# Attention and mixer on one core: half-width transform matmuls grouped, mixer engines kept in written order, MLP pieces rearranged

## The chip, the cores and the metric

The kernel runs on one core of a Trainium2 chip. The metric is device time in microseconds (us), from launch to the last output. Engines are named as the profile names them: PE (TensorE matmul), PEld (its weight load), DVE (VectorE), ACT (ScalarE), POOL (GpSimd) and SP (SyncE, which here only issues DMAs).

## The reference

Eight images of 128 x 128 pixels and 64 channels, float32, pass two layers.

```python
# layer 0: attention along the rows and columns of each pixel
Q, K, V = x @ w_q, x @ w_k, x @ w_v                  # Q, K: 8 channels
att = softmax(concat([Q.K along h (self masked), Q.K along w]))
x = gamma * (att_H V + att_W V) + x
# layer 1: Fourier mixer, then a convolutional MLP
F  = fft2(LN(x) @ w_te)                              # 64 -> 128 channels
fc = gelu(concat([F.re, F.im]) @ w_fc)
x1 = x + real(ifft2(fc.re + 1j * fc.im)) @ w_tp
h2 = LN(x1) @ w_fe                                   # 64 -> 128 channels
d  = gelu(depthwise_conv3x3(h2) + b_dw)
out = x1 + d @ w_fp
```

## The kernel before

**Two stages.** `attention` runs all eight images and writes its result to DRAM; `mixer` runs after it. The change is in the mixer.

**One image in the mixer.** `fourier(b)` transforms image b and leaves x1 in SBUF; `mlp(b)` makes the output from x1. While image b is transformed, the MLP of image b-1 runs beside it; image 0 has no MLP beside it, and the MLP of image 7 runs alone at the end. `fourier` yields after each of 36 steps of three kinds:

- W, 8 steps: transform along w for 8 channels (matmuls `aps`, L487) and a copy to `at` (ACT, L488).
- K, 19 steps over 17 groups of frequencies. Step i transforms group i along h (matmuls into `fps`, L499 to L507, copy `f` on ACT, L509), multiplies group i-1 by the channel weights (`fcps`, L522; gelu on ACT, L528; add or subtract on POOL, L529), and projects group i-2 back to 64 channels (`gps`, L549; copy `gt` on ACT, L552). Fifteen groups have 4 frequencies, one has 3, and the last holds the two real ones, 0 and 64.
- I, 9 steps over 8 blocks of 8 channels: inverse along h (`inverse_h`: matmuls `yps`, L576 to L580, copy `ys` on ACT, L581), then one step later inverse along w (`inverse_w`: matmuls `dps`, L587, and two additions into x1 on DVE, L593).

**A complex product.** For each frequency or channel one matmul has a full-width stationary operand of 128 columns (real and imaginary part of 64 channels) and two have half-width operands of 64 columns, which write the lower and the upper half of the partitions. A float32 matmul appears in the trace as two passes, so one such triple is six rows of PE.

**The MLP** goes through 16 chunks of 8 image rows. Of chunk k: `normed(k)` (POOL, L618), `transposed(k)` (four PE transposes `tpn`, L627, and an ACT copy `xtn`, L631), `expand(k)` (matmuls `hp`, L648, and ACT copies `h`, L642 and L653), nine `taps` of the 3x3 filter (tap 0 on ACT, L670; taps 1 to 8 on DVE, L672, all into one accumulator `acc`), `gelu(k)` (ACT, L679) and `shrink(k)` (POOL adds the bias to x1 in `ot`, L690; 8 matmuls `op`, L695; DVE adds them, L696; SP sends `ot` out, L697). `statistics(s)` takes mean and variance of 64 rows on DVE (L612) and ends with a square root on ACT (L71) and a reciprocal on DVE (L72). The MLP is a generator too; each `yield` ends a piece.

**What sets the order.** The main loop calls `next` on the MLP in proportion to the work done:

```python
        pieces = 4 + PIECES * (P // CH)
        work = W_STEP * 8 + K_STEP * (len(groups) + 2) + I_STEP * 9
        ...
                    while share < pieces * done / work:
                        next(before, None)
```

With weights 2, 7 and 5 the work of an image is 194, so a K step is followed by about three pieces and an I step by about two. After each I step two pieces of `load_norm(b+1)` follow (DMA `xl`, L470, and POOL `xn`, L471). This written order is not what the engines get: a scheduler reorders the instructions of every engine by its own estimate of when they are ready.

**Buffers.** PSUM in the mixer: two buffers for `fps`, `gps` and `yps`, two for `aps`, `fcps` and `dps`, and two (`ps_c`) for `tpn`, `op` and the two halves of `hp`. In SBUF most tiles have two buffers; `xn`, `at` and `gt` share two.

Of the kernel before, what the change touches and what calls it, by code (L numbers as in the profile page):

```python
# [21 lines left out]
F32 = mybir.dt.float32  # L22
BF16 = mybir.dt.bfloat16
AF = mybir.ActivationFunctionType
ALU = mybir.AluOpType
# [4 lines left out]
P = 128  # L30
C = 64
# [3 lines left out]
CH = 8  # L35
NORM_ROWS = 8

W_STEP, K_STEP, I_STEP = 2.0, 7.0, 5.0
PIECES = 5


def dft_tables():
# [321 lines left out]
def mixer(tc, nc, x2, scale1, tbl, prm, out):  # L364
# [3 lines left out]
    with ExitStack() as ctx:  # L368
# [111 lines left out]
        def fourier(b):  # L480
# [11 lines left out]
            for g in groups + [None, None]:  # L492
                nxt = None
                if g is not None:
                    fps = ps_m.tile([P, 4, P], F32, tag="mm", name="fps")
                    for n, k in enumerate(g):
                        if k % 64 == 0:
                            a = at[:, k // 64, :]
                            nc.tensor.matmul(fps[0:64, n, :], lhsT=a, rhs=cos, start=True, stop=True)  # L499
                            nc.tensor.matmul(fps[64:128, n, :], lhsT=a, rhs=nsin, start=True, stop=True)  # L500
                            continue
                        nc.tensor.matmul(  # L502
                            fps[:, n, :], lhsT=at[:, 2 * k : 2 * k + 2, :].rearrange("p t c -> p (t c)"), rhs=cos,
                            start=True, stop=False,
                        )
                        nc.tensor.matmul(fps[0:64, n, :], lhsT=at[:, 2 * k + 1, :], rhs=sin, start=False, stop=True)  # L506
                        nc.tensor.matmul(fps[64:128, n, :], lhsT=at[:, 2 * k, :], rhs=nsin, start=False, stop=True)  # L507
                    f = p2.tile([P, 4, P], F32, tag="f", name="f")
                    nc.scalar.copy(f[:, 0 : len(g), :], fps[:, 0 : len(g), :])  # L509
                    nxt = (g, f)  # L510
                tp_next = None
                if pend_fc is not None:
                    gg, f = pend_fc
                    n = len(gg) * P
                    fv = f.rearrange("p k h -> p (k h)")[:, 0:n]
                    gs = []
                    for half in range(2):
                        ps = ps_f.tile([P, 2, 512], F32, tag="fc", name="fcps")
                        cols = slice(half * HID, half * HID + HID)
                        for sgn, w in enumerate((wplus, wminus)):  # L520
                            mean = gg[0] == 0
                            nc.tensor.matmul(ps[:, sgn, 0:n], lhsT=w[:, cols], rhs=fv, start=True, stop=not mean)  # L522
                            if mean:
                                nc.tensor.matmul(
                                    ps[:, sgn, 0:1], lhsT=dc[:, cols], rhs=ident[0:1, 0:1], start=False, stop=True
                                )
                        gl = p2.tile([P, 2, 512], F32, tag="gl%d" % half, name="gl")
                        nc.scalar.activation(gl[:, :, 0:n], ps[:, :, 0:n], AF.Gelu, bias=bfc[:, half : half + 1])  # L528
                        nc.gpsimd.tensor_tensor(  # L529
                            gl[:, 0, 0:n], gl[:, 0, 0:n], gl[:, 1, 0:n], ALU.add if half == 0 else ALU.subtract  # L530
                        )
                        gs.append(gl)
                    tp_next = (gg, gs)
                if pend_tp is not None:
                    gg, (gr, gi) = pend_tp
                    gps = ps_m.tile([P, 4, 2, C], F32, tag="mm", name="gps")
                    if gg[0] == 0:

                        nc.tensor.matmul(gps[:, 0, 0, :], lhsT=gr[:, 0, 0:P], rhs=wtp, start=True, stop=False)
                        nc.tensor.matmul(gps[:, 0, 0, :], lhsT=gi[:, 0, P : 2 * P], rhs=wtpn, start=False, stop=False)  # L540
                        nc.tensor.matmul(gps[:, 0, 0, :], lhsT=e0, rhs=btp, start=False, stop=True)
                        nc.tensor.matmul(gps[:, 0, 1, :], lhsT=gi[:, 0, 0:P], rhs=wtp, start=True, stop=False)
                        nc.tensor.matmul(gps[:, 0, 1, :], lhsT=gr[:, 0, P : 2 * P], rhs=wtp, start=False, stop=True)
                        k0, n = 63, 1
                    else:
                        k0, n = gg[0] - 1, len(gg)
                        for j in range(n):
                            for t, src in enumerate((gr, gi)):
                                nc.tensor.matmul(  # L549
                                    gps[:, j, t, :], lhsT=src[:, 0, j * P : j * P + P], rhs=wtp, start=True, stop=True  # L550
                                )
                    nc.scalar.copy(gt[:, :, :, k0 : k0 + n], gps[:, 0:n, :, :].rearrange("p k t c -> p c t k"))  # L552
                pend_fc, pend_tp = nxt, tp_next
                yield K_STEP
# [15 lines left out]
        def inverse_h(gt, c0):  # L570
            ys = p2.tile([P, 8, P], F32, tag="ys", name="ys")
            for g in range(2):
                yps = ps_m.tile([P, 4, P], F32, tag="mm", name="yps")
                for n in range(4):
                    c = c0 + 4 * g + n
                    nc.tensor.matmul(  # L576
                        yps[:, n, :], lhsT=gt[:, c, :, :].rearrange("p t k -> p (t k)"), rhs=cos, start=True, stop=False
                    )
                    nc.tensor.matmul(yps[0:64, n, :], lhsT=gt[:, c, 1, :], rhs=nsin, start=False, stop=True)  # L579
                    nc.tensor.matmul(yps[64:128, n, :], lhsT=gt[:, c, 0, :], rhs=sin, start=False, stop=True)  # L580
                nc.scalar.copy(ys[:, 4 * g : 4 * g + 4, :], yps)  # L581
            return ys

# [18 lines left out]
        def mlp(b):  # L602
# [75 lines left out]
                av = accs[k][:, 0 : i1 - i0, :]  # L678
                nc.scalar.activation(av, av, AF.Gelu)  # L679

            def shrink(k):
                i0, i1 = span(k)
                acc = accs.pop(k)
                for a in range(0, i1 - i0, CH):
                    n = min(CH, i1 - i0 - a)
                    r0 = k * CH - 1 + i0 + a
                    ot = p2.tile([P, CH, C], F32, tag="ot", name="ot")
                    for o, rows in lines(xs, r0, r0 + n):
                        m = rows.shape[1]
                        nc.gpsimd.tensor_tensor(  # L690
                            ot[:, o : o + m, :], rows, bfp.unsqueeze(1).to_broadcast([P, m, C]), ALU.add
                        )
                    op = ps_c.tile([P, CH, C], F32, tag="mc", name="op")
                    for i in range(n):
                        nc.tensor.matmul(op[:, i, :], lhsT=acc[:, a + i, :], rhs=wfp, start=True, stop=True)  # L695
                    nc.vector.tensor_tensor(ot[:, 0:n, :], op[:, 0:n, :], ot[:, 0:n, :], ALU.add)  # L696
                    nc.sync.dma_start(  # L697
                        out=out[b, r0 : r0 + n, :, :].rearrange("h w c -> w h c"), in_=ot[:, 0:n, :]
                    )

            statistics(0)
            normed(0)
            normed(1)
            yield
            transposed(0)
            yield
            expand(0)
            taps(0, 0, 1)
            yield
            for k in range(n_ch):  # L710
                taps(k, 1, 4)
                yield
                if k > 0:
                    gelu(k - 1)
                if k == 4:
                    statistics(1)
                if k + 2 < n_ch:
                    normed(k + 2)
                yield
                taps(k, 4, 6)  # L720
                if k > 0:
                    shrink(k - 1)
                yield
                if k + 1 < n_ch:
                    transposed(k + 1)
                taps(k, 6, 9)
                yield
                if k + 1 < n_ch:
                    expand(k + 1)
                    taps(k + 1, 0, 1)  # L730
                yield
            gelu(n_ch - 1)
            shrink(n_ch - 1)
            yield

        pieces = 4 + PIECES * (P // CH)
        work = W_STEP * 8 + K_STEP * (len(groups) + 2) + I_STEP * 9
        for _ in load_norm(0):  # L740
            pass
# [19 lines left out]
def attention_mixer_kernel(ctx: ExitStack, tc: tile.TileContext, x, w_q, b_q, w_k, b_k, w_v, b_v, gamma, *rest):  # L761
# [5 lines left out]
    keep = ctx.enter_context(tc.tile_pool(name="keep", bufs=1))  # L767
    scale1 = keep.tile([P, NB, P], F32, tag="scale1", name="scale1")
    attention(tc, nc, x, w_q, b_q, w_k, b_k, w_v, b_v, gamma, x2, scale1)
    mixer(tc, nc, x2, scale1, tbl, prm, out)  # L770


_INS = [
# [29 lines left out]
```

## Time and profile before

| | us |
|---|---|
| median of 3 runs (lowest to highest) | 4361.75 (4358.06 to 4362.67) |
| the profiled execution, its own time | 4356.02 |
| its span, first to last instruction | 4354.3 |
| attention, until the mixer's first DFT matmul (`aps`) | 1808.7 |
| image 0 in the mixer (first `aps` of image 0 to that of image 1) | 220.7 |
| a later image (first `aps` of image 2 to that of image 3) | 294.6 |
| image 7 and the last MLP, to the end | 557.0 |

The profiled execution is 5.7 us under the median of the runs. Busy shares over the whole span are PE 86%, DVE 63%, POOL 40%, ACT 38%, but they mix the two stages. A row of a timeline gives start, duration, engine, line and shape. Ends of matmuls are modelled, so the rate of PE is read from one start to the next. A wait in a list is the idle time of an engine and what ended it. "PEclk" is the share of the TensorE clock that was granted.

### The profile page before, as it was taken

What the parts mean: (1) busy time and instruction counts of PE and PEld (TensorE: products, weight loads), DVE (VectorE), ACT (ScalarE), POOL (GpSimd) and SP (SyncE); (2) the same over time, 40 slices, a digit from 0 to 9 for tenths busy, and PEclk for the clock granted to TensorE, in tenths of its full rate; (3) what the DMA queues carried; (4) which work ended last, traced back from release to release, by engine and by line L of the source; (5) the groups of instructions that cost most, each with busy time, mean ns of one, the idle gap of its engine ahead of it and who ended that gap; (6) DMA issues with size and microseconds to landing.
All of it is one profiled execution on the core that took longest, in us unless ns stands there. A gap on an engine that the chain in (4) does not pass through costs nothing.

```text
span 4354.3 us, 77800 instructions
## 1 busy us (share of the span) xinstructions
PE 3734.6 (86%) x32742; PEld 2615.0 (60%) x32742; DVE 2753.9 (63%) x4392; ACT 1672.0 (38%) x2215; POOL 1733.9 (40%) x1601
## 2 busy tenths in 40 slices
PE   7979797979897976499989989899899899899634
PEld 4665767666766665366656656566566566666423
DVE  4353545454545454104878878888878789788776
ACT  1405050505041412143635535536445355265222
POOL 0142424242424244333562554635725636344121
PEclk7859585858585857699989989999899899999755
DMA  3132322323232322401121111120211211200000
GB/s 91 44 106 56 105 78 83 89 72 96 67 101 60 100 56 67 144 6 35 37 54 32 37 51 35 51 57 15 73 35 35 54 34 42 61 14 16 13 17 20
DMA packets 452064, 243.92 MB, mean 56 GB/s; under 512 B 415874, under 2 KB 420354, under 8 KB 445570
## 3 DMA queue, kind: packets, MB, share of 16 engines
q1 hardware_dynamic: 439426, 205.37, 17.5%
q0 software_dynamic: 12288, 33.57, 2.1%
q8 instruction: 258, 4.23, 0.4%
q14 instruction: 92, 0.75, 0.1%
HBM read 169.66 MB, written 68.16 MB: 55 GB/s over the span
## 4 chain that ended last, share of the span: by engine, by line
PE 62%; DVE 13%; POOL 12%; DMA 6%; issue 4%; ACT 1%; SPq 1%; POOLq 0%; DVEq 0%; ACTq 0%
PE fcps L522 8%; PE e L200 7%; DVE acc L672 6%; PE op L695 5%; PE yps L576 4%; DMA xr<-in_x_dram 4%; PE gps L549 4%; PE yps L579 4%; PE fps L502 4%; PE pq L169 4%; PE fps L506 4%; POOL yo L340 3%; PE zp L275 3%; PE zp L261 3%; PE sp L284 3%
## 5 line engine op out<-in xcount | busy, mean ns | idle before, releaser
L672 DVE SCALAR_TENSOR_TENSOR acc<-h,wdw,acc 128x1024 f32<-128x1024 f32 (+2 forms) x1024 | 1604.3, 1597 | 104.0 <-ACT acc L670 86.2
L529 POOL TENSOR_TENSOR gl<-gl 128x512 f32<-128x512 f32 (+2 forms) x272 | 478.1, 1767 | 450.4 <-ACT gl L528 450.4
L340 POOL TENSOR_TENSOR yo<-yo,xr 128x512 f32<-128x512 f32 x128 | 162.2, 1267 | 703.7 <-DVE yo L336 703.3
L695 PE MATMUL op<-wfp,acc 128*128 128x64 f32 x2048 | 288.6, 302 | 140.7 <-ACT acc L679 140.0
L690 POOL TENSOR_TENSOR ot<-x,bfp 128x512 f32<-128x512 f32 (+1 forms) x144 | 215.3, 1500 | 465.9 <-DMA out_dram<-ot 413.7
L695 PEld LDWEIGHTS op<-wfp,acc 128*128 128x128 f32 x2048 | 279.7, 218 | 185.6 <-ACT acc L679 176.4
L528 ACT ACTIVATE gl<-fcps,bfc 128x1024 f32<-128x1024 f32 (+2 forms) x272 | 291.9, 1074 | 153.5 <-PE fcps L522 149.2
L245 ACT ACTIVATE att<-e 128x1024 f32<-128x1024 f32 x256 | 249.0, 1021 | 223.2 <-PE e L200 223.1
L593 DVE TENSOR_TENSOR x<-dps,x 128x512 f32<-128x512 f32 x128 | 85.1, 684 | 340.1 <-DMA xl<-x 216.6
L549 PEld LDWEIGHTS gps<-wtp,gl 128*128 128x128 f32 x2016 | 249.2, 194 | 71.1 <-issue 53.1
L522 PE MATMUL fcps<-f,wplus 128*128 128x512 f32 (+2 forms) x544 | 283.1, 602 | 0.0
L200 PE MATMUL e<-ktH,qtH 8*128 8x128 f32 x2048 | 202.3, 445 | 92.2 <-DVE negH L214 90.8
L471 POOL TENSOR_TENSOR xn<-xl,scale 128x512 f32<-128x512 f32 x128 | 253.1, 1987 | 44.3 <-DMA xl<-x 43.8
L522 PE MATMUL fcps<-f,wminus 128*128 128x512 f32 (+2 forms) x544 | 270.1, 578 | 0.0
L261 PE MATMUL zp<-att,xh 128*64 128x64 f32 x4096 | 182.0, 257 | 97.2 <-POOL att L247 73.8
L344 DVE BATCH_NORM_STATS2 stats<-yo 128x6 f32<-128x64 f32 x1024 | 143.9, 211 | 188.7 <-POOL yo L340 188.6
L549 PE MATMUL gps<-wtp,gl 128*128 128x64 f32 x2016 | 247.5, 275 | 13.1 <-POOL gl L529 13.1
L618 POOL TENSOR_TENSOR xc<-x,scale 128x512 f32<-128x512 f32 x128 | 174.2, 1366 | 206.7 <-PE tpn L627 170.7
L225 ACT COPY jt<-tw 128x128 f32<-128x128 f32 x8 | 2.1, 265 | 648.6 <-PE tw L223 648.6
L247 POOL TENSOR_SCALAR_AFFINE_SELECT att<-att 128x1024 f32<-128x1024 f32 x128 | 137.4, 1092 | 283.2 <-ACT att L245 283.2
L576 PE MATMUL yps<-tb,gt 128*128 128x128 f32 x1024 | 249.6, 326 | 0.5 <-ACT gt L552 0.5
L200 PEld LDWEIGHTS e<-ktH,qtH 8*128 8x128 f32 x2048 | 183.5, 320 | 110.6 <-DVE negH L214 106.0
(147 smaller groups left out, 7424.5 us busy)
## 6 DMA issues: line engine op xcount, KB each, us to landing
xw<-in_x_dram SPq DMA_DIRECT2D x256, 128.0 KB
xr<-in_x_dram SPq DMA_DIRECT2D x256, 128.0 KB
xh<-in_x_dram SPq DMA_DIRECT2D x32, 1024.0 KB
x<-yo POOLq DMA_DIRECT2D x256, 128.0 KB, 2.5
x<-x SPq DMA_DIRECT2D x16, 2048.0 KB
xl<-x SPq DMA_DIRECT2D x128, 256.0 KB
out_dram<-ot SPq DMA_DIRECT2D x120, 256.0 KB
sd<-ss SPq DMA_DIRECT2D x128, 8.0 KB
```

Of the source, the lines that this page charges most:

```text
L200: nc.tensor.matmul(es[q // 2][:, q % 2, i, :], lhsT=o.qk[d, lhs][part, 4 * r + i, :], rhs=o.qk[d, rhs][part, 4 * r + i, :], start=True, st ...
L245: nc.scalar.activation(att, e.rearrange("p q i w -> p (q i) w"), AF.Exp)
L261: nc.tensor.matmul(zp[64 * s : 64 * s + 64, n, :], lhsT=o.xh[:, w, :], rhs=att.rearrange("p n (h s) -> p n s h", s=2)[:, n, s, :], start=T ...
L340: nc.gpsimd.tensor_tensor(yo, yo, xr, ALU.add)
L471: nc.gpsimd.tensor_tensor(xn[:, :, h : h + NORM_ROWS], xl.rearrange("p h c -> p c h"), scale1[:, b, h : h + NORM_ROWS].unsqueeze(1).to_bro ...
L522: nc.tensor.matmul(ps[:, sgn, 0:n], lhsT=w[:, cols], rhs=fv, start=True, stop=not mean)
L528: nc.scalar.activation(gl[:, :, 0:n], ps[:, :, 0:n], AF.Gelu, bias=bfc[:, half : half + 1])
L529: nc.gpsimd.tensor_tensor(gl[:, 0, 0:n], gl[:, 0, 0:n], gl[:, 1, 0:n], ALU.add if half == 0 else ALU.subtract)
L549: nc.tensor.matmul(gps[:, j, t, :], lhsT=src[:, 0, j * P : j * P + P], rhs=wtp, start=True, stop=True)
L576: nc.tensor.matmul(yps[:, n, :], lhsT=gt[:, c, :, :].rearrange("p t k -> p (t k)"), rhs=cos, start=True, stop=False)
L672: nc.vector.scalar_tensor_tensor(out=av, in0=src, scalar=wdw[:, t : t + 1], in1=av, op0=ALU.mult, op1=ALU.add)
L695: nc.tensor.matmul(op[:, i, :], lhsT=acc[:, a + i, :], rhs=wfp, start=True, stop=True)
```

## The change

1. In `fourier`, the four full-width matmuls of a group come first, then the four pairs of half-width ones. In `inverse_h` the same. The start flag[...] stands only on the first matmul of a group, and the stop flag on the last.
2. The mixer is wrapped in a block that keeps the written order on PE, DVE, ACT and POOL. SP's DMA issues are still placed by the scheduler.
3. The MLP's pieces are cut anew. The statistics piece is followed by five empty pieces (`LEAD = 6`); an image has 89 pieces instead of 84. Within a chunk's five pieces `gelu(k-1)` and `transposed(k+1)` move to the first, `shrink(k-1)` to the second, `expand(k+1)` and `normed(k+2)` to the fourth, tap 0 of the next chunk to the fifth. `shrink` is split: matmuls and the POOL addition in piece 2, the DVE addition and the DMA out in a new function `store`, in piece 3.

```diff
+LEAD = 6
...
+                    real = g[0] == 0
                     for n, k in enumerate(g):
...
+                        if not real:
+                            nc.tensor.matmul(
+                                fps[:, n, :], lhsT=at[:, 2 * k : 2 * k + 2, :].rearrange("p t c -> p (t c)"), rhs=cos,
+                                start=n == 0, stop=False,
+                            )
+                    for n, k in enumerate(g):
+                        s_re, s_im = (k // 64, k // 64) if real else (2 * k, 2 * k + 1)
                         nc.tensor.matmul(
...
+                            fps[0:64, n, :], lhsT=at[:, s_im, :], rhs=cos if real else sin, start=real and n == 0, stop=n == len(g) - 1
                         )
...
+                        nc.tensor.matmul(fps[64:128, n, :], lhsT=at[:, s_re, :], rhs=nsin, start=real and n == 0, stop=n == len(g) - 1)
...
                 for n in range(4):
                     c = c0 + 4 * g + n
                     nc.tensor.matmul(
...
+                        yps[:, n, :], lhsT=gt[:, c, :, :].rearrange("p t k -> p (t k)"), rhs=cos, start=n == 0,
+                        stop=False,
+                    )
+                for n in range(4):
+                    c = c0 + 4 * g + n
+                    nc.tensor.matmul(yps[0:64, n, :], lhsT=gt[:, c, 1, :], rhs=nsin, start=False, stop=n == 3)
+                    nc.tensor.matmul(yps[64:128, n, :], lhsT=gt[:, c, 0, :], rhs=sin, start=False, stop=n == 3)
...
-            def shrink(k):
+            def shrink(k, a):
...
+                op = ps_c.tile([P, CH, C], F32, tag="mc", name="op")
+                for i in range(n):
+                    nc.tensor.matmul(op[:, i, :], lhsT=accs[k][:, a + i, :], rhs=wfp, start=True, stop=True)
+                return r0, n, ot, op
+
+            def store(r0, n, ot, op):
+                nc.vector.tensor_tensor(ot[:, 0:n, :], op[:, 0:n, :], ot[:, 0:n, :], ALU.add)
+                nc.sync.dma_start(out=out[b, r0 : r0 + n, :, :].rearrange("h w c -> w h c"), in_=ot[:, 0:n, :])
 
             statistics(0)
             normed(0)
             normed(1)
-            yield
+            for _ in range(LEAD):
+                yield
             transposed(0)
             yield
             expand(0)
+            yield
             taps(0, 0, 1)
-            yield
             for k in range(n_ch):
-                taps(k, 1, 4)
-                yield
                 if k > 0:
                     gelu(k - 1)
+                if k + 1 < n_ch:
+                    transposed(k + 1)
                 if k == 4:
                     statistics(1)
-                if k + 2 < n_ch:
-                    normed(k + 2)
+                taps(k, 1, 3)
                 yield
-                taps(k, 4, 6)
-                if k > 0:
-                    shrink(k - 1)
+                held = shrink(k - 1, 0) if k > 0 else None
+                taps(k, 3, 5)
                 yield
-                if k + 1 < n_ch:
-                    transposed(k + 1)
-                taps(k, 6, 9)
+                if held:
+                    store(*held)
+                taps(k, 5, 6)
                 yield
                 if k + 1 < n_ch:
                     expand(k + 1)
+                if k + 2 < n_ch:
+                    normed(k + 2)
+                taps(k, 6, 8)
+                yield
+                if k + 1 < n_ch:
                     taps(k + 1, 0, 1)
+                taps(k, 8, 9)
                 yield
             gelu(n_ch - 1)
-            shrink(n_ch - 1)
+            for a in (0, CH):
+                store(*shrink(n_ch - 1, a))
             yield
...
-        pieces = 4 + PIECES * (P // CH)
+        pieces = LEAD + 3 + PIECES * (P // CH)
...
-    mixer(tc, nc, x2, scale1, tbl, prm, out)
+    E = mybir.EngineType
+    with tc.manual_schedule(engines={E.PE, E.DVE, E.Activation, E.Pool}):
+        mixer(tc, nc, x2, scale1, tbl, prm, out)
```

## The prediction, made before the run

> **What bounds the kernel now.** I read the page first (busy shares, slices), then windows cut at the first `aps` of images, then PE's and DVE's waits inside one image, then single rows of PE and of DVE's tail.
>
> ```profile
> span 4354.3 us, 77800 instructions
> PE 3734.6 (86%) x32742; PEld 2615.0 (60%) x32742; DVE 2753.9 (63%) x4392; ACT 1672.0 (38%) x2215; POOL 1733.9 (40%) x1601
> ```
>
> Windows of the mixer: image 0 alone; image 2 with the MLP of image 1; image 7; the last MLP alone (start:end, length, busy by engine, granted clock):
>
> ```profile
> 1808.70:2029.40 220.70, 219.09 (x1336) 142.30 (x1337) 9.02 (x14) 74.59 (x93) 64.91 (x50) 0.99 0.08 22
> 2324.30:2618.90 294.60, 277.11 (x1722) 183.90 (x1721) 244.01 (x300) 145.12 (x193) 145.93 (x118) 0.96 0.16 44
> 3797.30:4082.40 285.10, 275.67 (x1721) 182.86 (x1719) 236.25 (x303) 145.20 (x193) 113.27 (x103) 0.98 0.09 24
> 4082.40:4354.30 271.90, 110.33 (x402) 78.23 (x402) 199.02 (x288) 74.42 (x100) 52.30 (x66) 0.50 0.07 17
> ```
>
> Image 0 is all PE. In a later image PE is busy 277 of 294.6 us, DVE 244. The waits of image 2, PE's and then DVE's:
>
> ```profile
> PE gps L539 <- POOL gl L529: 8.0, 1, 8.0
> PE gps L540 <- POOL gl L529: 3.4, 1, 3.4
> PE gps L549 <- POOL gl L529: 2.1, 1, 2.1
> ...
> DVE ot L696 <- PE op L695: 16.9, 6, 12.1
> DVE acc L672 <- ACT acc L670: 12.1, 7, 3.6
> ```
>
> PE waits once, 13.5 us at the end of the K steps, because POOL has put `xn` of the next image ahead of the last `gl`; the clock is then at half for 24 us. Otherwise PE never stops: it is the bound. In the tail the clock is 0.50 and DVE has 73 us of idle, in this rhythm (an addition, 15 taps, an addition, one tap, idle):
>
> ```profile
> 4197.36 0.69 DVE L696 TENSOR_TENSOR ot<-op,ot 128x512 f32<-128x512 f32 x1 [7.11 <-issue]
> 4197.97 20.19 DVE L672 SCALAR_TENSOR_TENSOR acc<-h,wdw,acc 128x1024 f32<-128x1024 f32 x15
> ...
> 4228.23 0.69 DVE L696 TENSOR_TENSOR ot<-op,ot 128x512 f32<-128x512 f32 x1 [7.11 <-issue]
> ```
>
> That is 30.9 us for two chunks, 8.2 of them idle (7.1 and 1.1).
>
> [...] The trace: waits of 4.5 us or more halved it (in attention, for about 17 to 20 us), waits of 2.1 did not by themselves. [...] a tap is 1.28 us beside an idle POOL, but 15 taps take 24.14 us (1.61 each) in the K steps. [...]
>
> **Part 1, the grouped matmuls.** One old triple of PE's timeline (two full passes, two pairs of half passes; L580's rows left out), and below it the group of frequencies 0 and 64, which already has four pairs in a row:
>
> ```profile
> 2253.13 0.49 PE L576 MATMUL yps<-tb,gt 128*128 128x128 f32 x2
> 2253.55 0.32 PE L579 MATMUL yps<-tb,gt 128*64 128x128 f32 x1
> ...
> 2253.71 0.27 PE L579 MATMUL yps<-tb,gt 128*64 128x128 f32 x1
> ...
> 2253.92 0.49 PE L576 MATMUL yps<-tb,gt 128*128 128x128 f32 x2
> ```
>
> The four pairs in a row:
>
> ```profile
> 2212.24 0.32 PE L499 MATMUL fps<-tb,at 128*64 128x128 f32 x1
> ...
> 2212.40 0.27 PE L499 MATMUL fps<-tb,at 128*64 128x128 f32 x1
> ...
> 2212.51 0.27 PE L499 MATMUL fps<-tb,at 128*64 128x128 f32 x1
> ...
> 2212.62 0.27 PE L499 MATMUL fps<-tb,at 128*64 128x128 f32 x1
> ...
> 2212.83 0.91 PE L522 MATMUL fcps<-f,wplus 128*128 128x384 f32 x2
> ```
>
> A triple takes 0.79 us, a group 3.15. After a switch the first pair takes 0.16, the next 0.11 each, the last 0.21 up to the full-width one. Full passes in a row take 0.112 each (`aps`: 16 in 1.79); the last before a switch 0.205. A new group is 7 x 0.112 + 0.205 + 0.16 + 6 x 0.107 + 0.203 = 2.0, or 2.1 where it follows a half-width one. Each image has 32 groups: 31 x 1.07 + 0.8 (the group of three) = 34 us less PE work. A K step falls from 3.15 + 3.43 (`fcps`) + 1.79 (`gps`) = 8.4 to 7.3.
>
> In **image 0** nothing else is near: ACT is busy 75 us, POOL 65, and `xn` of image 1 arrived at 4.25 us a pair against 6.0 us for a new I step. Worth **-34 us**, whole.
>
> **Parts 2 and 3, a later image.** The order listing of the changed kernel shows on ACT: tap 0 of the next chunk, gelu of the last, `xtn`, then the three kinds of copies of K steps, all in one line; PE takes `op` behind that gelu, and the second `hp` waits for DVE's `store`, whose PSUM buffer it takes over. I walked one image by hand, t = 0 where DVE starts the statistics:
>
> - W: statistics 8.3 (64 in the tail's rows: 26 in 3.39, 38 in 4.91) + deviation 0.8; ACT's root stands behind one `at` copy and ahead of six, so `aps` stops after three blocks until 10.4; then five blocks, `tpn`, `hp`: PE enters K1 at 21. `h`, `f` and tap 0 follow: DVE's first tap at 25, 15 us idle. The five empty pieces cost nothing.
> - K: three steps per two chunks (3.2 pieces per step). Along PE and ACT: op 1.8, K step 7.3, hp 1.1, tpn 0.4, K step 7.3, op 1.8, wait for store 1.5 (behind four taps, and behind POOL's `ot`, now after two `gl`), hp 1.1, K step 7.3, then gt 0.6, tap 0 1.2, gelu 1.1 with 0.3 of handing over: 32.8 us, 10.9 per step. DVE does 16 x 1.61 + 2 x 0.61 = 27 in it, and waits about 3.9 for that tap 0, 1.5 for `op`. K1 and K2 take 10.7, K3 to K16 14 x 10.9 = 153, statistics(1) 6 beyond the idle time they fill, K17 to K19 24: 194, so I1 starts at 215. POOL's `xn` now stand behind the last `gl`: the 13.5 us stall goes.
> - I: DVE is the bound. It lags 5; 4.1 chunks of 13.5 + 1.6 (the ninth row) + 16 x 0.61 for additions + 3 waiting for `dps` + 5 for the last gelu, `op` at half clock (PE has idled 10 us) and stores: 80 in all, so 294. The moved DMAs: SP sends `xl` in fours between two stores. A store can be held 5 to 11 us until `xn` frees an `xl`; `ot` is needed again two chunks (27 us) later, so no cost. `normed` is moved two pieces and has a chunk of slack.
>
> **294 against 294.6**: the 34 us of PE and the 13.5 us stall turn into waits of the fixed order. Six such images: -4 us.
>
> **The last MLP.** In the fixed order each chunk's `op` runs under the next chunk's taps: gelu 1.1 + op 3.7 (half clock) = 4.8, before the store's turn at 5.4; hp, `h`, tap 0 end at 9.2, before the chunk's 8 x 1.35 + 0.61 = 11.4 are over. So DVE does not wait: 16.8 to the first tap, 16 chunks 183, statistics(1) 11, last gelu, op, store, DMA 9.7 (3.7 of it the DMA, as now): 220. Image 7 and this are 294 + 220 = 514 against 557.0: **-43 us**.
>
> **Sum.** 4356.0 - 34 - 4 - 43 = 4275 for a profiled execution. The median before was 5.7 above its profiled execution; I add 4: **4279**. With P the period, the change is 7P - 2139 us: break-even is P = 305.5. My own range for this case is P from 284 to 304, 4205 to 4345.
>
> **Rivals.**
> 1. *DVE becomes the only bound.* If the waits of the K steps fall away, P is DVE's 244 + 15 + 8 (start and end gaps) = 267: 4356 - 34 - 6 x 28 - 70 = 4084. For it: DVE's work leaves 50 us of room. Against: tap 0 stands behind `gt` in the listing in every second chunk. Chance 0.14.
> 2. *The clock.* PE's waits for `op` in the K steps are some 2.6 to 3.3 us in my walk; at 4.5 us the clock falls. Each fall (17 to 24 us at half) delays PE by about 8. It decides from two falls per image on (P over 305.5); three give P = 318, 4443. For it: 8 us waits did it in each image before. Against: waits of 2.1 alone did not, and W's `aps` refill at once. Chance 0.19.
> 3. *The switch is not saved*[...]: image 0 gains nothing, P is near 314, 4449. Against: the four L499 rows. Chance 0.05.
>
> The walked case has 0.62, and 0.04 of it lies within 0.2%, which is what a measurement of this kernel can tell from no change. Faster 0.73, same 0.05, slower 0.22. The range, 4160 to 4385, takes the lower half of rival 1's way and the start of rival 2's.
>
> **What would show it.** Right: `yps` groups of about 2.1 us; image 0 at 187; no PE wait for `gl` at the end of K; DVE waiting for tap 0 (L670's successor) some 4 us in every second chunk; a tail of 220 with DVE nearly full. Wrong: a period under 284 (the fixed order costs less than I walked), half clock inside the K steps (rival 2), or a tail with idle DVE.

## The result, and the profile after

The changed kernel takes 4535.06 us (4531.97 to 4535.73), the kernel before 4359.91 (4351.92 to 4362.67), four runs of each: a ratio of 1.0403, 95% interval 1.0385 to 1.0421. It is **slower by 4%**; the forecast was 4279, faster by 2%, with a range of 4160 to 4385.

The page's head, and below it the windows of the four stages (start:end, length, busy by engine, granted clock, DMA):

```profile
span 4534.0 us, 77769 instructions
...
PE 3801.3 (84%) x32742; PEld 2789.6 (62%) x32742; DVE 2672.1 (59%) x4392; ACT 1685.4 (37%) x2217; POOL 1609.6 (35%) x1601
```

```profile
1801.60:1989.40 187.80, 186.20 (x1337) 137.21 (x1338) 9.02 (x14) 74.67 (x93) 65.49 (x50) 0.99 0.09 25
2319.40:2649.90 330.50, 287.51 (x1722) 209.16 (x1722) 231.12 (x300) 146.67 (x193) 129.44 (x118) 0.86 0.14 39
3978.70:4289.30 310.60, 281.89 (x1703) 204.55 (x1703) 209.76 (x293) 145.19 (x192) 90.29 (x101) 0.87 0.06 14
4289.30:4534.00 244.70, 141.04 (x403) 86.08 (x402) 217.79 (x292) 77.82 (x102) 62.41 (x69) 0.51 0.09 20
```

Image 0 is 33 us shorter than before, as forecast. Image 2 is 36 us longer, at a clock of 0.86 instead of 0.96. PE is busy 10 us more than before, though the grouping took 34 us of passes away: that is the oddity to explain. The last MLP alone is 27 us shorter.

From profile to profile: attention 7.1 us shorter (the code is the same), image 0 32.9 shorter, the six later images 221.5 longer (1989.3 against 1767.8), image 7 and the last MLP 1.7 shorter: 179.8 us together, and the two spans differ by 179.7. The loss lies in the later images.

PE's and DVE's longest waits in image 2 (what waited, for what: us in total, times, longest):

```profile
PE op L700 <- ACT acc L685: 24.2, 9, 8.2
PE tpn L633 <- POOL xc L624: 8.3, 5, 4.3
...
DVE acc L678 <- ACT acc L676: 62.2, 11, 17.3
DVE ot L704 <- POOL ot L695: 14.8, 4, 5.0
```

The stall for POOL's last `gl` (13.5 us before) is gone. In its place `op` waits for gelu nine times, and DVE waits for tap 0 in eleven places.

The windows of one cycle of two chunks and three K steps show what a short wait brings. They are cut where the clock changes, and where the first `op` starts:

```profile
2474.00:2480.70 6.70, 5.51 (x29) 3.44 (x27) 6.28 (x4) 4.52 (x7) 3.35 (x3) 1.00 0.00 0
2480.70:2482.10 1.40, 1.40 (x13) 1.40 (x13) 0.76 (x1) 0.41 (x1) 1.40 (x1) 0.98 0.00 0
2482.10:2485.50 3.40, 3.40 (x20) 3.17 (x20) 2.23 (x3) 0.00 (x0) 0.52 (x1) 0.50 0.22 51
2485.50:2495.70 10.20, 7.82 (x46) 4.60 (x42) 3.88 (x4) 6.62 (x9) 4.86 (x6) 1.00 0.05 10
2495.70:2502.50 6.80, 6.21 (x32) 5.98 (x34) 6.59 (x7) 1.01 (x2) 0.00 (x0) 0.50 0.05 12
2502.50:2512.00 9.50, 9.50 (x65) 6.24 (x62) 3.83 (x3) 5.97 (x8) 3.62 (x5) 1.00 0.09 20
```

The clock column reads 1.00, 0.98, 0.50, 1.00, 0.50, 1.00. PE is idle 1.19 + 2.38 + 0.59 = 4.2 us of the 38. In the two stretches at 0.50 it is busy 3.40 + 6.21 us and gets about half of that done (the 16 passes of `op` take 3.47 us from 2496.29 to the next row, and 1.88 from 2538.38, at full clock): 4.8 us lost. What is left, 38.0 - 4.2 - 4.8 = 29.0, is the work at full clock. The forecast's list for such a cycle has 28.1 us of PE's work (it counts one of the two `tpn`) and 4.7 of waits, 32.8: **both came out within 1 us, and 4.8 of the 5.2 us of the miss are clock**. The cycle shown is a usual one: K steps 3 to 16 of image 2 took 175.3 us, 37.6 for three.

**A table for the experiments.** The same sum for a mean later image (first `aps` of image 2 to that of image 7, by five). The ratio is to the kernel before as measured together with each kernel (its medians were 4357.59 to 4359.97). Idle is the length less PE's busy time. Lost is half of PE's busy time in the stretches with a granted clock of 0.5, an estimate from the two times of `op` above. Rest is what remains; as ends of matmuls are modelled, I trust it to some 10 us, 240 to 250 for grouped matmuls, 271 to 275 for triples.

| kernel | median us | ratio (95% interval) | later image | idle | lost | rest |
|---|---|---|---|---|---|---|
| before | 4359.91 | 1 | 294.6 | 17 | 7 | 271 |
| the change | 4535.06 | 1.0403 (1.0385 to 1.0421) | 331.8 | 43 | 43 | 247 |
| grouped_only | 4300.02 | 0.9862 (0.9843 to 0.9882) | 294.7 | 33 | 21 | 240 |
| no_fixed | 4285.99 | 0.9818 (0.9793 to 0.9842) | 291.5 | 22 | 20 | 250 |
| fixed_only | 4812.21 | 1.1039 (1.1010 to 1.1067) | 362.4 | 34 | 55 | 274 |
| filler | 4470.66 | 1.0250 (1.0230 to 1.0270) | 320.9 | 29 | 15 | 277 |
| not_grouped | 4900.21 | 1.1241 (1.1224 to 1.1257) | 376.2 | 36 | 66 | 275 |
| tap0_early | 4504.60 | 1.0330 (1.0310 to 1.0350) | 327.1 | 38 | 43 | 247 |
| normed_early | 4541.46 | 1.0418 (1.0402 to 1.0433) | 331.4 | 41 | 44 | 247 |
| op_late | 4517.64 | 1.0354 (1.0313 to 1.0394) | 324.5 | 41 | 34 | 250 |
| grouped_fixed | 4468.49 | 1.0246 (1.0204 to 1.0288) | 318.6 | 39 | 35 | 245 |
| filler_k | 4712.01 | 1.0809 (1.0785 to 1.0834) | 350.8 | 41 | 36 | 274 |
| no_fixed_filler | 4310.56 | 0.9894 (0.9863 to 0.9924) | 298.6 | 20 | 17 | 261 |
| fixed_mended | 4443.71 | 1.0194 (1.0170 to 1.0217) | 317.1 | 28 | 24 | 264 |
| tail_fixed | 4245.12 | 0.9739 (0.9720 to 0.9759) | 290.9 | 22 | 19 | 250 |
| group_k | 4696.15 | 1.0786 (1.0761 to 1.0812) | 348.5 | 37 | 51 | 261 |
| group_i | 4742.72 | 1.0886 (1.0849 to 1.0923) | 357.0 | 41 | 56 | 261 |

### The profile page after: what moved, and what is told of

The parts are those of the page before. It is cut to its first block, busy times and chain, and to the rows that moved or that the text cites. A ratio compares the mean times of both kernels' runs of the same rounds, so it can differ in the third digit from the quotient of the medians.

```text
span 4534.0 us, 77769 instructions
## 1 busy us (share of the span) xinstructions
PE 3801.3 (84%) x32742; PEld 2789.6 (62%) x32742; DVE 2672.1 (59%) x4392; ACT 1685.4 (37%) x2217; POOL 1609.6 (35%) x1601
## 5 line engine op out<-in xcount | busy, mean ns | idle before, releaser
L678 DVE SCALAR_TENSOR_TENSOR acc<-h,wdw,acc 128x1024 f32<-128x1024 f32 (+2 forms) x1024 | 1521.6, 1488 | 488.5 <-ACT acc L676 453.4
L532 POOL TENSOR_TENSOR gl<-gl 128x512 f32<-128x512 f32 (+2 forms) x272 | 377.1, 1390 | 1090.7 <-ACT gl L531 1090.2
L700 PE MATMUL op<-wfp,acc 128*128 128x64 f32 x2048 | 338.0, 335 | 226.7 <-ACT acc L685 226.7
L700 PEld LDWEIGHTS op<-wfp,acc 128*128 128x128 f32 x2048 | 319.9, 246 | 259.7 <-ACT acc L685 258.5
L654 PE MATMUL hp<-xtn,wfe 64*128 64x512 f32 x512 | 263.9, 732 | 55.9 <-ACT h L659 39.5
L525 PE MATMUL fcps<-f,wplus 128*128 128x512 f32 (+2 forms) x544 | 302.7, 640 | 0.0
L659 ACT ACTIVATE h<-hp,bfe 128x512 f32<-128x512 f32 x256 | 170.5, 690 | 283.5 <-PE hp L654 283.2
```

The source lines that it names most:

```text
L532: nc.gpsimd.tensor_tensor(gl[:, 0, 0:n], gl[:, 0, 0:n], gl[:, 1, 0:n], ALU.add if half == 0 else ALU.subtract)
L654: nc.tensor.matmul(hps[s].rearrange("p j w -> p (j w)"), lhsT=wfe[half, :], rhs=xt[half, :, :].rearrange("p j w -> p (j w)"), start=True, ...
L678: nc.vector.scalar_tensor_tensor(out=av, in0=src, scalar=wdw[:, t : t + 1], in1=av, op0=ALU.mult, op1=ALU.add)
L700: nc.tensor.matmul(op[:, i, :], lhsT=accs[k][:, a + i, :], rhs=wfp, start=True, stop=True)
```

## The experiments

**My theory** after the result: the written order makes PE wait a little, often, and each such wait throws PE to half clock (a fall of the clock, below) for longer than the wait lasted. **Rivals**: the waits alone cost the time; PE's mean density decides the clock, wherever its work lies; the new pieces, not the fixed order, are at fault.

### The parts one by one

**grouped_only**: the kernel before with part 1 alone.

> The kernel before with part 1 alone (grouped matmuls; scheduler's order and old pieces stay). If the saving of 34 us of PE per image is real and the fixed order is what costs time, this kernel gains: image 0 about 188 us instead of 220.7, a later image between 262 (DVE's work and its gaps) and 280, the tail as before, so about 4130 to 4250 us in all. If grouping itself makes later images slow, by freeing PE into waits at half clock, it is above 4360.

Measured: 4300.02 us. Image 0 took 188.2 us, 32.5 less than before. A later image took 294.7, no less than before. Image 2 has this row of windows:

```profile
2282.55:2578.80 296.25, 263.12 (x1721) 191.75 (x1720) 244.60 (x300) 144.51 (x193) 149.18 (x118) 0.90 0.16 43
```

Image 0 is as expected; a later image and the total lie between the two sides. What follows: the grouping is real, and where PE alone sets the time (image 0) it pays in full. In a later image PE's rest falls by 31 us and all of it comes back, 16 as idle time and 15 as clock. Even the scheduler's order does not hold this gain.

**fixed_only** (the kernel before with part 2 alone) and **no_fixed** (the change without part 2).

```diff
-    mixer(tc, nc, x2, scale1, tbl, prm, out)
+    E = mybir.EngineType
+    with tc.manual_schedule(engines={E.PE, E.DVE, E.Activation, E.Pool}):
+        mixer(tc, nc, x2, scale1, tbl, prm, out)
```

> The kernel before with part 2 alone (order kept as written, old pieces, old matmul order). If the fixed order is what costs, this is slower than before by more than the changed kernel is, because neither the 34 us of grouping nor the new pieces help: a later image above 331 us, 4600 to 5000 in all. If the new pieces are what costs, it is at or below 4360, because the 13.5 us wait for POOL goes.

> The changed kernel without the block that fixes the order (parts 1 and 3: grouped matmuls and new pieces). If the fixed order makes the waits, a later image falls from 331 us to 262 to 285 and the whole to 4100 to 4260. If it is the new cut of the pieces that makes them, for instance tap 0 behind a whole K step, it stays above 4400.

Measured: fixed_only 4812.21, as its theory had it; no_fixed 4285.99, just above its theory's 4260 and far below the rival's 4400. A row and a wait of one image of no_fixed:

```profile
2865.90:3156.50 290.60, 269.29 (x1722) 190.15 (x1722) 247.13 (x300) 144.89 (x193) 151.89 (x118) 0.92 0.16 44
```

```profile
PE op L700 <- ACT acc L685: 3.7, 1, 3.7
```

What follows: the fixed order is what makes the kernel slower. It costs 249 us on parts 1 and 3 (4535 against 4286), 452 on the kernel before. In the scheduler's order `op` waits for gelu once in this image (3.7 us), in the fixed order nine times (24.2).

**not_grouped** (parts 2 and 3) and **grouped_fixed** (parts 1 and 2).

> Parts 2 and 3 without part 1 (fixed order, new pieces, matmuls ungrouped): 34 us more PE work per image. Theory (the cycle of waits gelu, op, store, hp, tap 0 sets a later image, and thin PE work lets the clock fall): image 0 goes back to 221, a later image grows by less than 34 us, to 335 to 350, because the added passes fill waits and hold the clock up; mean clock of a later image above 0.86; median 4600 to 4710. Rival (PE's work is the path and the waits only add to it): every later image grows by the full 34 us, to 365, median 4535 + 33 + 7 x 34 = 4806, near that of the fixed order with the old pieces (4812).

> Parts 1 and 2 without part 3: the fixed order and the grouping with the old pieces. So far: fixed order with old pieces, ungrouped, 361.8 us per later image; with new pieces, ungrouped, 375; with new pieces, grouped, 331. Theory (the parts are worth about the same with and without each other: the grouping takes some 44 us off a later image in the fixed order, the new pieces add 13 to it): a later image takes 312 to 322, median 4420 to 4490. Rival (the new pieces are bad only with dense PE work; where the grouping has thinned it, their earlier gelu and later store help): a later image takes over 331, median above 4540.

Measured: not_grouped 4900.21, 376.2 us per later image; grouped_fixed 4468.49, 318.6. For not_grouped both sides were wrong: an image grows by 44 us, more than the 34 us of work, and the median lies above even the rival's 4806. The added passes took only 7 us off the idle time, and lost time grew from 43 to 66. grouped_fixed fell in the range of its theory. What follows: in the fixed order the grouping is worth 44 us an image with either set of pieces (362.4 to 318.6 and 376.2 to 331.8), and the new pieces cost 13 to 14 us an image with or without it. In the scheduler's order the new pieces make a difference of 14 us in all (4300 and 4286), with intervals that just meet. So the new pieces are a part of the loss, 67 us of the whole (4535 against 4468), but without them the fixed order is still 2.5% slower than the kernel before (grouped_fixed).

### Which of the waits matters

**tap0_early**, **normed_early** and **op_late** each move one step of the fixed order:

```diff
 # tap0_early: tap 0 in the fourth piece instead of the fifth
                     expand(k + 1)
+                    taps(k + 1, 0, 1)
...
-                if k + 1 < n_ch:
-                    taps(k + 1, 0, 1)
 # normed_early: xc in the first piece instead of the fourth
                     transposed(k + 1)
+                if k + 2 < n_ch:
+                    normed(k + 2)
 # op_late: op in the third piece, store at the start of the fourth
-                held = shrink(k - 1, 0) if k > 0 else None
                 taps(k, 3, 5)
                 yield
-                if held:
-                    store(*held)
+                held = shrink(k - 1, 0) if k > 0 else None
                 taps(k, 5, 6)
                 yield
+                if held:
+                    store(*held)
```

> Tap 0 of the next chunk moves from the fifth piece into the fourth, right behind expand: no K step's copies can stand between h and tap 0 on ACT any more. Theory (DVE's 62 us per image of waiting for tap 0 belong to the cycle that sets a later image): DVE's wait for ACT's acc falls to under 25 us, gelu and op come earlier, PE's waits for op (24 us) fall with it and the clock rises; a later image takes 300 to 318 instead of 331, median 4320 to 4445. Rival (DVE has slack, it waits because PE is late with hp): the DVE wait turns into another wait of DVE, a later image stays at 328 to 333.

> The POOL multiplication xc of chunk k+2 moves from the fourth piece into the first, ahead of the addition ot. Theory (tpn's wait for xc is a small part of the cycle): PE's waits tpn<-POOL xc, 8.3 us per image, vanish, and each was followed by a stretch at half clock; a later image takes 315 to 325, median 4420 to 4490. Rival (what is saved at tpn is lost at op, which waits for gelu anyway, or ot comes later and store and hp wait for it): a later image stays at 328 to 333, with DVE's wait for ot (14.8 us) longer.

> The matmuls op and the addition ot move from the second piece to the third, store from the third to the start of the fourth, ahead of hp. Theory (op waits because it stands too close behind the taps and the gelu, and these waits drop the clock): PE's waits op<-ACT acc fall from 24 us to under 10 and the time at half clock from 92 to under 60 us; hp now stands behind store, which costs up to 2 us per chunk; a later image takes 305 to 320, median 4350 to 4460. Rival (the cycle is only rotated: what op no longer waits for, hp waits for behind store): PE's waits move to hp, a later image 328 to 340, clock unchanged.

Measured, in image 2: tap0_early takes DVE's wait for tap 0 from 62.2 to 48.2 us and the image from 330.5 to 324.9; lost time stays at 42. normed_early takes PE's wait for `xc` from 8.3 to 1.7, but `hp` then waits 5.6 instead of 2.1 for DVE's `store`; the image stays (331.2). DVE's wait for `ot`, which the rival expected to grow, fell to 10.3. op_late takes PE's wait for gelu from 24.2 to 16.2 and time at half clock from 92 to 83; the image takes 324.9.

What follows: no single misplaced step explains 37 us. normed_early was the rival's case in its time; the other two lay between the sides, tap0_early (327.1 in the mean) next to its rival: they give 5 and 7 us an image.

### Waits or clock

**filler**: the changed kernel with two full matmuls of 128x512 ahead of each `op`. They write the tile that `op` then overwrites, so PE computes while `op`'s gelu is still under way.

```diff
                 op = ps_c.tile([P, CH, C], F32, tag="mc", name="op")
+                for _ in range(2):
+                    nc.tensor.matmul(op.rearrange("p r c -> p (r c)"), lhsT=idw, rhs=tb[:, 0:512], start=True, stop=True)
```

> The changed kernel with two matmuls of 128x512 more (0.86 us each at full clock) into the PSUM tile of op, ahead of the eight real ones, which overwrite them; they need only the buffer, so PE does them while it would wait for the gelu. They add 17 x 1.7 = 29 us of PE work per image. If the half clock that follows the waits costs the time, the granted clock in the K steps rises from 0.85 towards 0.95 and a later image falls from 331 us to 305 to 322 (4400 to 4490 in all). If the waits alone cost it and the clock costs nothing because PE has slack, a later image is 331 to 350 and the total 4535 to 4670.

**filler_k**: the same 34 matmuls per image, but inside the `fcps` block of the K steps, where PE has no wait (0.0 us of idle ahead of `fcps` on the changed kernel's page).

```diff
                             mean = gg[0] == 0
+                            if sgn == 0:
+                                nc.tensor.matmul(ps[:, sgn, 0:n], lhsT=w[:, cols], rhs=fv, start=True, stop=True)
```

> The changed kernel with the same extra PE work as the filler run (34 matmuls of 128x512 per image, their result overwritten), but inside the K step's fcps block, where PE is dense already, not ahead of op. Theory A (the clock falls where a wait leaves a stretch of PE thin; only a filler that lies in the wait helps): the waits for op and the time at half clock stay (20 to 30 us, and 80 to 100 us), a later image takes 350 to 365, median 4680 to 4790. Rival B (the mean density of PE's work decides the clock, wherever the work lies): time at half clock falls to some 40 us as in the filler run, a later image takes 315 to 330, median 4430 to 4540.

Image 2 and PE's wait for gelu, first of filler:

```profile
2305.10:2625.82 320.72, 291.52 (x1790) 201.86 (x1790) 233.63 (x299) 146.78 (x193) 135.77 (x118) 0.94 0.15 40
```

```profile
PE op L702 <- ACT acc L685: 9.0, 6, 6.5
```

and of filler_k:

```profile
2375.05:2727.07 352.02, 310.57 (x1790) 217.88 (x1790) 225.61 (x300) 146.70 (x193) 123.35 (x118) 0.88 0.13 37
```

```profile
PE op L702 <- ACT acc L687: 24.2, 9, 8.2
```

Both have 1790 rows of PE instead of 1722. In filler the clock is 0.94 and the image is 10 us shorter than the change's; in filler_k the clock is 0.88, the wait is as long as without it, and the image is 22 us longer (the kernels: 4471 and 4712 us). What follows: it is not PE's mean density that decides, against rival B; work that lies in the wait keeps the clock up. filler fell in its theory's range. In the mean image of filler the rest grew by 30 us, and idle fell by 13 and lost time by 27, which more than paid for it. Two thirds of what it undoes is clock, which the rival "waits alone" leaves out. filler_k lies at the low edge of theory A's range: 27 us of added work, 7 us less lost.

**no_fixed_filler** puts one such matmul ahead of `op` in the scheduler's order; **fixed_mended** joins tap0_early, op_late and one such matmul in the fixed order.

> Parts 1 and 3 in the scheduler's order, with one 128x512 matmul ahead of each op (15 us more PE work per later image). Without it a later image takes 290.7 us: some 249 of work at full clock, 20 lost at half clock, 21 idle. Theory (the clock eats what the grouping saves): the time lost at half clock falls by 10 or more and the idle by 5, so the 15 us added cost nothing: 286 to 291 per later image, median 4255 to 4290. Rival (in the scheduler's order waits are few and the filler only adds work): 300 to 306, median 4350 to 4395.

> The changed kernel in its fixed order with three edits: tap 0 of the next chunk in the fourth piece, op one piece later with store at the start of the fourth piece, and one 128x512 matmul ahead of each op. Alone, the first two gave 327 and 324 us per later image, two fillers 320.8. Theory (the edits act on different waits and add up, and the filler keeps the clock up): 305 to 315, median 4350 to 4425, so still slower than or equal to the kernel before: the fixed order cannot be mended by small moves. Rival (with op late there is nothing left for the filler to fill): 322 to 335, median 4470 to 4560.

Measured: no_fixed_filler 4310.56 us and 298.6 per later image, slower than no_fixed. My theory missed there, and the image lies next to its rival's. Its lost time fell by 3 us and its idle by 2, against 12 of added work: `op` hardly waits in the scheduler's order (3.7 us in the image of no_fixed above), so the matmul has little to fill. (Its last MLP was 25 us shorter than that of no_fixed, at a mean clock of 0.66 instead of 0.51; no run tests that by itself.) fixed_mended came to 4443.71 and 317.1, between the two sides: the edits add up in part, and it stays 1.9% slower than the kernel before.

### How long a fall lasts, and the last MLP

The ungrouped kernels wait less than the change and lose more, so the wait alone does not set the length of a fall. **group_k** groups only the `fps` of the K steps, **group_i** only the `yps` of the I steps; in each the other kind keeps its triples. **tail_fixed** has the scheduler's order everywhere but in the last MLP:

```diff
         for b in range(NB + 1):
...
+            if b == NB:
+                E = mybir.EngineType
+                with tc.manual_schedule(engines={E.PE, E.DVE, E.Activation, E.Pool}):
+                    for _ in before:
+                        pass
             for rest in (before, after):
...
-    E = mybir.EngineType
-    with tc.manual_schedule(engines={E.PE, E.DVE, E.Activation, E.Pool}):
-        mixer(tc, nc, x2, scale1, tbl, prm, out)
+    mixer(tc, nc, x2, scale1, tbl, prm, out)
```

> The changed kernel with only the fps matmuls of the K steps grouped; the yps of the I steps stay as triples (17 us more PE work per later image than in the changed kernel). Ungrouped, a later image lost 66 us at half clock with 36 us of idle, grouped 41 with 43: the same waits cost more. Theory A (a fall ends only when PE's own work lets it, and a triple with its switches keeps the clock down, wherever it stands): one long fall of some 50 us in the I steps as in the ungrouped kernel, short ones of 3.4 to 6.8 us in the K steps; lost about 52, later image 340 to 350, median 4610 to 4700. Theory B (only the length of the wait sets the length of the fall): lost 40 to 45, later image about 345 minus 10, 330 to 338, median 4540 to 4610.

> The changed kernel with only the yps matmuls of the I steps grouped; the fps of the K steps stay as triples. Theory A (a triple keeps the clock down wherever it stands): the long fall in the I steps is 27 us or less, the falls in the K steps 6.8 to 13.7 us; lost about 54, later image 340 to 352, median 4610 to 4710. Theory B (only the wait's length counts): lost 40 to 45, later image 330 to 338, median 4540 to 4610.

> Parts 1 and 3 in the scheduler's order for attention and all eight transforms; the written order is kept (part 2) only for the last MLP, which runs alone. Theory (the written order is right where PE has no transform beside the MLP, and wrong where it has): image 0 and the later images as in the scheduler's order (188 and 291 us), the time after the last dps falls from 274.7 to 245 us as in the changed kernel, median 4250 to 4266. Rival (the tail gained only because the work of image 7's MLP lay differently when it began): the tail stays over 265, median 4276 to 4290.

Measured for the falls. In these two kernels each of images 2 to 6 has one long fall where the last K step meets the first I steps. The windows that hold just this fall in image 2, first of group_k, then of group_i:

```profile
2589.60:2640.80 51.20, 48.62 (x182) 32.02 (x182) 29.50 (x19) 12.38 (x19) 22.99 (x18) 0.50 0.18 47
```

```profile
2613.70:2641.00 27.30, 24.72 (x90) 17.73 (x89) 20.66 (x15) 9.63 (x14) 13.53 (x13) 0.50 0.15 38
```

With triples in the I steps it lasts 51.2 us (15 windows of 3.41) in four of the five images of group_k and in all five of not_grouped, and 27.3 in one; grouped it lasts 23.9 or 27.3 us in all five of group_i and of the change. Ahead of it stands each time one and the same wait of 0.8 us. With the old pieces it is 37.5 to 41.0 us in fixed_only and 13.7 in grouped_fixed, behind a wait of 1.5 us in both. In the K steps it is the other way round: the commonest fall in the image lasts 3.4 us in group_k and 10.2 us in group_i. group_k fell in theory A's range of medians; group_i (4742.72) and its image (357.0) lie above A's. B's values are out for both. What follows: **after the same wait, the form of PE's own work sets how long a fall lasts, and triples make it longer**. Image 0, with no MLP beside it, agrees: behind one wait of 0.5 us its clock fell for 23.9 us in fixed_only and group_k, whose `yps` are triples, and for 3.4 us in filler, whose `yps` are grouped. So the grouping is worth 44 us an image in the fixed order instead of 34: lost time falls with it, from 66 to 43. What in a triple does it, the switches or something else, no run separates. Why image and kernel of group_i are dearer than expected is not settled; its images take 351 to 364 us.

For tail_fixed, image 2, image 7, and the last MLP, and below them the last MLP of no_fixed:

```profile
2273.60:2564.00 290.40, 269.07 (x1721) 189.95 (x1721) 246.98 (x300) 144.89 (x193) 152.85 (x118) 0.92 0.16 44
3728.00:3999.50 271.50, 258.36 (x1721) 183.11 (x1719) 233.77 (x300) 144.77 (x193) 112.03 (x99) 0.97 0.09 24
3999.50:4240.10 240.60, 141.06 (x403) 86.11 (x402) 217.03 (x291) 77.79 (x102) 61.93 (x68) 0.51 0.08 19
```

```profile
4012.00:4286.70 274.70, 123.13 (x402) 86.07 (x402) 200.92 (x291) 75.20 (x100) 42.05 (x65) 0.51 0.07 17
```

The later image is that of no_fixed, and the last MLP takes 240.6 us instead of 274.7. 4245.12 us is 5 below the expected range and the best of all kernels here: **2.6% faster than the kernel before**. The gain of the last MLP belongs to the written order there, where no transform runs beside it.

## Why the prediction was wrong, point by point

**Part 1, right.** A group in image 0 of the changed kernel (start, duration, row; a new group begins at the next L579):

```profile
1963.88 1.05 PE L579 MATMUL yps<-tb,gt 128*128 128x128 f32 x8
1964.87 0.32 PE L585 MATMUL yps<-tb,gt 128*64 128x128 f32 x1
...
1965.89 1.16 PE L579 MATMUL yps<-tb,gt 128*128 128x128 f32 x8
```

2.01 us to the next group, 2.12 for the one behind it; forecast 2.0 and 2.1. Image 0: 187.8, forecast 187. Rival 3 is out. Fewer changes between full and half width took 33 us from image 0, with the same weight loads (1338 rows, 1337 before). What a change spends its time on is not shown.

**Parts 2 and 3, a later image: wrong, 331.6 us in the mean of six instead of 294.** The forecast's term that failed is the K step, "10.9 us per step", and with it the "24" for K17 to K19: waits were priced by their length, and PE was taken at full clock behind them. The first `yps` of image 2 came 246.9 us after the statistics began, not 215. Of these 32 us, 16 lie in K3 to K16 (175.3 us against 153 and 6 for the second statistics), 10 in K17 to K19 (33.6 against 24), 4 in K1 and K2, and 2 in W. PE lost 21 us at half clock in K3 to K16 and 10 in K17 to K19. The I steps took 83 us instead of 79 (its list for them adds up to 80). Six such images give 225 of the 261 us by which the sum (4275) missed the profiled execution (4535.73).

Behind the term stands a reading of the trace before, that waits of 2.1 us "did not by themselves" halve the clock. **That reading was wrong.** These are PE's rows around the stall for `gl` in image 2 before the change, and two windows of 3.4 us:

```profile
2519.43 1.80 PE L549 MATMUL gps<-wtp,gl 128*128 128x64 f32 x10 [2.12 <-POOL gl L529]
2529.22 0.69 PE L539 MATMUL gps<-wtp,gl 128*128 128x64 f32 x2 [7.99 <-POOL gl L529]
```

```profile
2516.70:2520.10 3.40, 1.28 (x10) 1.12 (x11) 3.37 (x2) 1.64 (x2) 3.40 (x3) 1.00 0.27 77
2520.10:2523.50 3.40, 1.13 (x6) 0.94 (x5) 3.29 (x3) 1.44 (x2) 3.40 (x2) 0.50 0.02 5
```

The clock fell at 2520.1, just behind the wait of 2.12 us; the wait of 8.0 began only at 2521.2. Images 2 to 6 are alike in this: each fall comes during the wait of 2.0 to 2.1 us or just behind it, and ahead of the long one. The forecast's own waits for `op`, 2.6 to 3.3 us, were longer than that.

**Rival 2 is what came, with another size.** It expected falls of 17 to 24 us, each worth 8 us, two or three an image, and for waits of 4.5 us or more. There were 13.2 an image in the mean, 59 of 66 not over 10.2 us, and together they lost 43 us. I had given it 0.19. In images 2 to 6 the falls of every kernel here are whole multiples of 3.41 us, and PE need not idle through such a window ahead of one: in the changed kernel windows with PE busy 2.63 of 3.41 us were followed by a fall.

**`normed`, "a chunk of slack": wrong but cheap.** PE waits 8.3 us for `xc`; taking most of it away left the image as long as it was (normed_early).

**The stall at the end of K, right.** The 13.5 us for `gl` are gone.

**The last MLP: the mechanism right, the size off.** DVE's rows there:

```profile
4407.20 11.95 DVE L678 SCALAR_TENSOR_TENSOR acc<-h,wdw,acc 128x1024 f32<-128x1024 f32 x8
4419.06 0.68 DVE L704 TENSOR_TENSOR ot<-op,ot 128x512 f32<-128x512 f32 x1
4419.67 11.84 DVE L678 SCALAR_TENSOR_TENSOR acc<-h,wdw,acc 128x1024 f32<-128x1024 f32 x8
```

DVE is full, as forecast, with no idle between chunks. But eight taps take 11.95 us, 1.49 each, where I had 1.35 from the tail before, in which DVE stood idle for 73 us. Now that DVE does not stop, more of POOL's `xc` and `ot` run beside taps. A tap of 128x1024 takes 1.28 us with POOL idle, before and after; beside POOL's work 40 of these 112 take 1.77 in the mean, where 32 took 1.59 before. From the statistics to the end it took 231.9 us, forecast 220.

**Image 7 and the last MLP: 555.3 instead of 514.** 12 of the 41 us are the taps; the rest is image 7, with the same falls of the clock as the others.

**Rival 1** (DVE the only bound) is out: DVE was busy 231 of 330 us.

## What to carry to other kernels

Price a short wait of PE by the clock as well as by its length. In images 2 to 6, of the waits that began at full clock, those of 1.5 us or more brought a fall, during the wait or within 3.41 us behind it, in 41 of 45 cases in the changed kernel, and in 5 of 5 before; those of 0.7 to 1.5 us in 34 of 50, and in none of 16 before. (One fall can stand behind two waits.) In images 2 to 6 of the changed kernel a fall cost at least 1.7 us, by the estimate of half of PE's busy time in it. After the same wait the fall was longer where the `yps` were triples (51.2 us in image 2 of group_k, 27.3 in that of group_i). An order written by hand should be tried for each stage by itself: here it cost 40 us an image where transforms ran beside the MLP (331.8 against 291.5) and saved 34 us where the MLP ran alone. Removing PE work in the scheduler's order paid in full where PE alone set the time (32.5 us in image 0 of grouped_only); beside a chain of other engines it came back as waits and clock (16 and 15 us of 31 in a later image).

## What the runs showed of the hardware

- The granted clock changes only at steps of 3.41 us. I laid a grid of such windows over images 2 to 6. In the changed kernel it fell 66 times, each time after a window in which PE was busy 2.63 us or less (median 1.71). It rose again 66 times, each time after a window in which PE was busy throughout (in other kernels after 2.7 us or more). Not every thin window brings a fall: windows with as little as 1.6 us of PE's time were followed by full clock.
- A busy window is no promise of the full clock. In not_grouped, 151 windows at half clock were followed by another at half clock, and the median of them was busy throughout. Dense triples alone need not cause a fall: image 0 before the change runs at 0.99 with them.
- A fall need not have a wait ahead of it. In attention, before the change, seven falls of 82 to 85 us each follow a window in which PE's only gaps are 0.2 us or less; most of its matmuls there read 8 partitions (`e`, 8x128). In image 0 of not_grouped a fall of 27.3 us follows a window of `gps` and `fcps` matmuls, most with 64 moving columns or fewer, in which PE was busy throughout. So the busy time in the trace is not all that counts; what else does is not shown.
- The same attention code took 1796 to 1811 us up to the first `aps` in the profiles of these kernels. A difference of a few microseconds between two kernels' spans has to be looked for in its stage first.
